# One graph network kernel: a tap step moved ahead of the first turn, input loads moved between queues, taps loaded three ahead, one copy moved to ScalarE

## The chip, the cores and the metric

The kernel runs on one core of one Trainium2 chip. The metric is the device time of one execution in microseconds. Below, PE is TensorE (matmuls and transposes), PEld its weight loads, DVE is VectorE, ACT is ScalarE, POOL is GpSimd, and SP is SyncE, which here only issues DMAs. "SPq" and "ACTq" in the profile are DMA issues of these two engines.

## The reference

The input is 128 graphs of 128 nodes with 256 features, `x (128, 128, 256)`, and an adjacency `adj (128, 128, 128)`. Two layers are computed. Cut to what matters:

```python
h  = relu(layernorm(x))                       # per node, over the 256 features
# layer 0, on every graph (channels are the features, the sequence is the nodes)
c1 = relu(bn1(conv1d(h, conv1_w)))            # 1 tap
xc = relu(bn2(conv1d(c1, conv2_w)) + h)       # 17 taps
A  = exp(-||se_i - se_j||^2) * adj            # se = h @ w_se.T + b_se
xn = A @ relu(h @ w_msg.T + b_msg)
i_r,i_z,i_n = split([xc, xn] @ w_ih.T + b_ih);  h_r,h_z,h_n = split(h @ w_hh.T + b_hh)
r, z = sigmoid(i_r + h_r), sigmoid(i_z + h_z)
x  = x + (1 - z) * tanh(i_n + r * h_n) + z * h
# layer 1
h  = relu(layernorm(x))
x  = x + sum over 5 groups g of nodes (all 25, and four subsets of them) of
         softmax(fusion_w)[g] * conv(conv(h[:, g], adj_g, W1[g], b1[g]), adj_g, W2[g], b2[g])
# conv(h, adj, W, b) = relu(D^-1/2 (adj + I) D^-1/2 (h @ W) + b), D the row sums (dinv = D^-1/2)
```

## The kernel before, in words

The graphs are cut into 32 blocks of four (`BB = 4`) and two halves of 16 blocks. The 17-tap convolution is done in a spectral form along the nodes: the taps are turned once into spectra (`vd` in DRAM), each half's activations are turned into spectra (the tile `X` in SBUF), both are multiplied per frequency, and the result (`yd`) goes to DRAM. One execution then has these stages, with the times of the profile before:

- **Heads of the first half together with the spectra of the taps, 0 to 173 us.** For each block `head_load` (L182) brings x in, `head_stats` takes mean and variance (DVE, L191 and L192; a power on POOL, L196), `head_norm` (DVE, L202) normalizes, `head_turn` transposes (eight PE transposes, L212, then relu on ACT into `ht`, L213, and a store of `ht` on the ACT queue, L214), `head_conv1` multiplies (PE, L226; add on DVE, L229; relu on ACT, L230) and `head_spectra` turns into spectra (PE, L241; copies into `X` on DVE, L247, and on ACT, L249). Between these steps `weight_spectra` runs. There are eight pieces of taps; each has four steps of 16 matmuls (two records each in the profile, L165) and four copies of the PSUM banks to the tile `sp`, three on ACT (L173) and one on DVE (L171; in the last step it is on ACT as well). After four steps `sp`, 2.56 MB, is stored to `vd` on the ACT queue (L175), and `some_spectra` starts the load of the taps after the next ones (1 MB, L155) on the ACT queue. The tile `w2` of the taps has two buffers, `sp` has two.
- **Spectral products of the first half, 173 to 277 us** (`spectral`). Per pair of frequencies p, two loads of 0.5 MB bring `v` from `vd` on SP (L294, three buffers); `s` is made on DVE (L307), `vs` on POOL (L309), then matmuls L312 and L317, and every four p a store of `yd` on the ACT queue.
- **Heads of the second half, 279 to 385 us, and its spectral products, to 489 us.**
- **The loop over blocks, to the end**: convolution output (L498 to L505), messages (L516 to L520), edges, `x_nmp` (L563 to L568), and the gates (PE, L612, by products of sums and differences of quarters: `t`, L586 to L589 for xn), with the second layer between them. The degree work of the second layer (`dinv`, L698 on) is on DVE at its start.

Order: in the first stage all engines follow the order of the text. After it SP and POOL still do, and the order of PE, DVE and ACT comes from a scheduler's cost model. DMAs signal on eight completion semaphores in turn, and an issue waits until the earlier DMA on its semaphore is complete.

`some_spectra()` does one step of 16 matmuls with its four copies. `constants()` computes the folded batch-norm vectors on DVE and POOL (L126 to L134) up to its first `yield`, and the matmuls L138 after it. `heads_begin` loads the first three blocks of the second half and takes their statistics; the generator is advanced at the frequencies p = 16, 24, 28 and so on of the first half's spectral products:

```python
        begin = heads_begin(hk, xk, 3, 1)
        amid = {p: lambda: next(begin, None) for p in range(16, NP_, 4) if p != 20}
        spectral(bp, X, 0, amid)
```

Its three loads were on the ACT queue, whose order is the scheduler's. In the profile they were issued at 142.33, 143.55 and 149.82 us, inside the heads of the first half.

Of the kernel before, what the change touches and what calls it, by code (L numbers as in the profile page):

```python
# [8 lines left out]
F32 = mybir.dt.float32  # L9
# [4 lines left out]
P = 128  # L14
# [8 lines left out]
WCH = 64  # L23
# [51 lines left out]
def gnn_kernel(ctx: ExitStack, tc: tile.TileContext, io, out0: bass.AP, out1: bass.AP):  # L75
    nc = tc.nc
# [15 lines left out]
    def bank():  # L92
        return psum.tile([P, 512], F32, tag="bank", name="bank")

    def row(name, n):

        return bass.AP(tensor=io[name].tensor, offset=io[name].offset, ap=[[0, P], [1, n]])
# [3 lines left out]
    vec = cst.tile([P, NV], F32)  # L101
# [10 lines left out]
    brz = cst.tile([P, 4], F32)  # L112

    def constant_loads():
        nc.sync.dma_start(vec, io["vec"])
        nc.sync.dma_start(wc1, io["wc1"].rearrange("(c p) o -> p c o", p=P))
        nc.sync.dma_start(fd, io["fd"])

# [30 lines left out]
    vd = dram.tile([C, D // WCH, P, LW, WCH], F32, tag="vd", name="vd")  # L149
    yd = [dram.tile([HG, 2, LW, D], F32, tag=f"yd{h}", name=f"yd{h}") for h in range(NH)]  # L150

    def taps_load(pool, c, q, queue, split=1):
        w2 = pool.tile([P, WCH // 4, P], F32, tag="w2", name="w2", bufs=2)
        for t in range(0, WCH // 4, WCH // 4 // split):
            queue.dma_start(w2[:, t:t + WCH // 4 // split], io["w2t"][:, c, q, t:t + WCH // 4 // split])  # L155
        return w2

    def weight_spectra(pool, c, q, w2):
# [21 lines left out]
    def head_load(pool, ahead, i, queue):  # L180
        xs[i] = pool.tile([P, BB, D], F32, tag="ln", name="ln", bufs=ahead)
        queue.dma_start(xs[i], x[i * BB:(i + 1) * BB].rearrange("b n d -> n b d"))  # L182

    def head_stats(wk, i, behind=None):

        mv = wk.tile([P, BB, 2], F32, tag="mv", name="mv", bufs=3)
        st = wk.tile([P, BB, 6], F32, tag="st", name="st", bufs=2)
        if behind is not None:
            nc.scalar.copy(st[:, :, 0], behind[:, :, 0])
        for b in range(BB):  # L190
            nc.vector.bn_stats(st[:, b, :], xs[i][:, b, :])  # L191
            nc.vector.bn_aggr(mv[:, b, :], st[:, b, :])  # L192
        ve = wk.tile([P, BB], F32, tag="ve", name="ve", bufs=2)
        nc.vector.tensor_scalar(ve, mv[:, :, 1], EPS, None, op0=ALU.add)  # L194
        rs = wk.tile([P, BB], F32, tag="rs", name="rs", bufs=3)
        nc.gpsimd.tensor_tensor(rs, ve, mhalf, op=ALU.pow)  # L196
        stats[i] = mv, rs
# [7 lines left out]
    def head_turn(wk, i):  # L205

        ln = xs.pop(i)
        ht = wk.tile([P, C, T], F32, tag="ht", name="ht", bufs=2)
        for c in range(C):
            ps = bank()  # L210
            for b in range(BB):
                nc.tensor.transpose(ps[:, b * N:(b + 1) * N], ln[:, b, c * P:(c + 1) * P], ident)  # L212
            nc.scalar.activation(ht[:, c, :], ps, AF.Relu)  # L213
        nc.scalar.dma_start(htd[i], ht)  # L214
        hcs[i] = ht
# [35 lines left out]
    def heads_begin(wk, xk, ahead, h):  # L251

        i = h * NBH
        for k in range(ahead):
            head_load(xk, ahead, i + k, nc.scalar)
        yield
        for k in range(3):
            head_stats(wk, i + k)
            yield
            if k < 2:  # L260
                head_norm(i + k)
        head_turn(wk, i)
# [80 lines left out]
    with front as es:  # L343
        hk = es.enter_context(tc.tile_pool(name="hk", bufs=1))
        xp = es.enter_context(tc.tile_pool(name="xp", bufs=1))
        X = xp.tile([P, C, NP_, 2, P], F32)
        order = es.enter_context(ExitStack())
        order.enter_context(tc.manual_schedule(engines={nc.gpsimd.engine}))
        sync_order = order.enter_context(ExitStack())
        sync_order.enter_context(tc.manual_schedule(engines={nc.sync.engine}))  # L350
        with ExitStack() as ws:

            ws.enter_context(tc.manual_schedule())

            xk = ws.enter_context(tc.tile_pool(name="xk", bufs=1, side="right"))
            wp = ws.enter_context(tc.tile_pool(name="wp", bufs=1))
            ahead = 5
            todo = [(c, q) for c in range(C) for q in range(D // WCH)]
            nc.scalar.dma_start(gt, io["gt"])
            taps = [taps_load(wp, *todo[0], nc.sync, split=4)]  # L360
            head_load(xk, ahead, 0, nc.scalar)
            spectra = []

            def some_spectra(k=1):
                for _ in range(k):
                    if not spectra and todo:
                        spectra.append(weight_spectra(wp, *todo.pop(0), taps.pop(0)))
                    if spectra and next(spectra[0], STOP) is STOP:
                        spectra.pop(0)
                        if len(todo) > 1:  # L370
                            taps.append(taps_load(wp, *todo[1], nc.scalar))
                        some_spectra()

            constant_loads()
            head_load(xk, ahead, 1, nc.sync)
            taps.append(taps_load(wp, *todo[1], nc.sync))
            for k in range(2, ahead):
                head_load(xk, ahead, k, nc.sync)
            nc.sync.dma_start(fw, row("fw", 5))
            head_stats(hk, 0)  # L380
            some_spectra()
            head_norm(0)
            some_spectra()
            head_turn(hk, 0)
            consts = constants()
            next(consts)
            some_spectra()
            head_stats(hk, 1)
            some_spectra()
            next(consts)  # L390
            head_norm(1)
            head_stats(hk, 2)
            some_spectra()
            heads(hk, xk, ahead, X, 0, some_spectra)
            while spectra or todo:
                some_spectra()
        gw = ctx.enter_context(tc.tile_pool(name="gw", bufs=1, side="right", reuse_waits="tile"))
        xk = es.enter_context(tc.tile_pool(name="xk1", bufs=1, reuse_waits="tile"))
        bp = es.enter_context(tc.tile_pool(name="bp", bufs=1, reuse_waits="tile"))
        idm = gw.tile([P, N], F32)  # L400
        wms = gw.tile([P, C, D + 3], F32)
        bms = gw.tile([P, D + 3], F32)
        wih = gw.tile([P, 2 * C, 3 * D], F32)
        whh = gw.tile([P, C, 3 * D], F32)
        sw = [gw.tile([P, 3, 3, P], F32, name=f"sw{k}") for k in range(3)]

        def small_loads():
            nc.sync.dma_start(idm, io["idm"])
            nc.sync.dma_start(wms, io["wms"].rearrange("(c p) o -> p c o", p=P))
            nc.sync.dma_start(bms, row("bms", D + 3))  # L410

        begin = heads_begin(hk, xk, 3, 1)
        sums = gate_weights()
        amid = {p: lambda: next(begin, None) for p in range(16, NP_, 4) if p != 20}
        spectral(bp, X, 0, amid)
        for _ in begin:
            pass

        def gate_loads():
            yield  # L420
            small_loads()
            yield
            yield
            nc.sync.dma_start(wih[:, :C], io["wih"][:D].rearrange("(c p) o -> p c o", p=P))
            yield
            yield
            nc.sync.dma_start(wih[:, C:], io["wih"][D:].rearrange("(c p) o -> p c o", p=P))
            yield
            yield
            nc.sync.dma_start(whh, io["whh"].rearrange("(c p) o -> p c o", p=P))  # L430

        loads = gate_loads()
        heads(hk, xk, 3, X, 1, lambda: next(loads, None))
        sync_order.close()
        spectral(bp, X, 1, {p: lambda: next(sums, None) for p in range(4, NP_, 4)})
        for _ in sums:
            pass
        order.close()
# [117 lines left out]
    def x_nmp(i):  # L556

        e, msg = A_s.pop(i), msgs.pop(i)
        xn = wk.tile([P, C, T], F32, tag="xn", name="xn", bufs=2)
        for c in range(C):  # L560
            ps = bank()
            for b in range(BB):
                nc.tensor.matmul(ps[:, b * N:(b + 1) * N], msg[:, b, c * P:(c + 1) * P], e[:, b, :],  # L563
                                 start=True, stop=True)
            if c:
                nc.vector.tensor_copy(xn[:, c, :], ps)  # L566
            else:
                nc.scalar.copy(xn[:, c, :], ps)  # L568
            yield
        xns[i] = xn  # L570
# [597 lines left out]
```

## Time and profile before

| | |
|---|---|
| time, median of 3 runs | 1918.53 us (1913.9 to 1918.58) |
| profiled execution: its own time | 1919.48 us |
| profiled execution: its span | 1917.7 us |
| PE busy | 1890.3 us (99% of the span) |
| DVE, ACT, POOL busy | 1303.9, 720.5, 609.1 us |
| granted PE clock, mean | 0.995 |
| DMA | 265.81 MB, 139 GB/s over the span |

The span is what the trace covers; the execution's own time is 1.8 us longer. "Busy" is the union of an engine's instructions. A line such as `L212 ... [2.63 <-issue]` says that the engine was idle for 2.63 us before this instruction, and what ended that idle time. "Chain" is the sequence of work and waits that is found by following back from the last instruction.

### The profile page before, as it was taken

The numbers are of one execution on the slowest core, as the hardware profiler recorded it, in microseconds if no ns is written. First come the engines' busy times: TensorE is split into PE (matmuls) and PEld (weight loads), VectorE is DVE, ScalarE is ACT, GpSimd is POOL, SyncE is SP. The second block draws the span as 40 slices with busy tenths as digits, with TensorE's granted clock in tenths as the row PEclk, the third lists the DMA queues.
The fourth block names the chain that finished last, engine by engine and source line by source line (L and its number), as shares of the span: only waits on it lengthen the run. The fifth ranks groups of instructions, "written<-read, shape, count | busy, mean of one in ns | idle before, by whom it ended". The sixth has DMA issues, their size and how long they took to land.

```text
span 1917.7 us, 30432 instructions
## 1 busy us (share of the span) xinstructions
PE 1890.3 (99%) x10610; PEld 1646.4 (86%) x10610; DVE 1303.9 (68%) x3247; ACT 720.5 (38%) x1555; POOL 609.1 (32%) x678
## 2 busy tenths in 40 slices
PE   8999999999999999999999999999999999999998
PEld 7888889988788888888888888888888888888887
DVE  5676557744677777777666677777756677787643
ACT  4553114411333343343343443333343434334334
POOL 1012531255234334433322233433322233443300
PEclk9999999999999999999999999999999999999999
DMA  8786896379842333333234433233334434222135
GB/s 322 288 312 226 297 311 235 121 241 306 256 117 73 74 95 76 81 90 106 71 94 97 130 97 87 73 82 108 75 90 97 144 72 107 65 78 71 36 92 151
DMA packets 248872, 265.81 MB, mean 139 GB/s; under 512 B 106866, under 2 KB 223943, under 8 KB 244239
## 3 DMA queue, kind: packets, MB, share of 16 engines
q1 hardware_dynamic: 236639, 196.70, 36.9%
q10 hardware_dynamic: 12080, 67.16, 9.0%
q8 instruction: 85, 1.39, 0.3%
q14 instruction: 68, 0.56, 0.1%
HBM read 178.66 MB, written 85.14 MB: 138 GB/s over the span
## 4 chain that ended last, share of the span: by engine, by line
PE 88%; DMA 4%; DVE 4%; issue 2%; ACT 1%; POOL 1%; SPq 0%; ACTq 0%; POOLq 0%; DVEq 0%
PE bank L612 45%; PE bank L317 6%; PE bank L516 5%; PE bank L937 5%; PE bank L877 5%; PE bank L226 4%; PE bank L312 3%; PE bank L563 3%; PE bank L498 3%; PE bank L241 3%; PE bank L165 2%; PE bank L501 1%; PE bank L788 1%; PE bank L856 1%; DMA v<-vd 1%
## 5 line engine op out<-in xcount | busy, mean ns | idle before, releaser
L612 PE MATMUL bank<-t,sw 128*128 128x256 f32 x1152 | 291.6, 380 | 0.7 <-DVE u L504 0.7
L625 POOL TENSOR_TENSOR u<-u,m 128x256 f32<-128x256 f32 x128 | 93.2, 728 | 612.7 <-ACT m L623 545.0
L612 PEld LDWEIGHTS bank<-t,sw 128*128 128x128 f32 x1152 | 215.8, 191 | 31.1 <-issue 2.3
L612 PE MATMUL bank<-t,wih 128*128 128x256 f32 x768 | 197.2, 379 | 0.0
L612 PEld LDWEIGHTS bank<-t,wih 128*128 128x128 f32 x768 | 143.4, 190 | 19.3 <-issue 0.5
L309 POOL TENSOR_TENSOR vs<-v 128x512 f32<-128x512 f32 x78 | 101.3, 1318 | 114.8 <-DMA v<-vd 49.4
L516 PE MATMUL bank<-wms,ht 128*128 128x259 f32 x512 | 124.1, 385 | 0.0
L226 PE MATMUL bank<-wc,ht 128*128 128x256 f32 x512 | 121.4, 391 | 1.6 <-ACT ht L213 1.6
L612 PE MATMUL bank<-xn,wih 128*128 128x256 f32 x384 | 114.9, 381 | 3.6 <-DVE xn L566 3.6
L612 PE MATMUL bank<-t,whh 128*128 128x256 f32 x384 | 115.0, 381 | 0.0
L612 PE MATMUL bank<-xc,wih 128*128 128x256 f32 x384 | 114.8, 381 | 0.0
L937 PE MATMUL bank<-w,hh 128*125 128x256 f32 (+9 forms) x480 | 113.5, 380 | 1.0 <-DVE hh L882 1.0
L226 PEld LDWEIGHTS bank<-wc,ht 128*128 128x128 f32 x512 | 98.0, 196 | 16.7 <-ACT ht L213 3.5
L516 PEld LDWEIGHTS bank<-wms,ht 128*128 128x128 f32 x512 | 98.3, 192 | 15.1
L612 PE MATMUL bank<-ht,whh 128*128 128x256 f32 x384 | 109.9, 380 | 0.0
L877 PE MATMUL bank<-ax,w 128*128 128x500 f32 (+8 forms) x416 | 107.0, 396 | 0.7 <-DMA w<-in_w_dram 0.7
L520 ACT ACTIVATE msg<-msg 128x512 f32<-128x512 f32 x64 | 40.3, 630 | 174.1 <-DVE msg L517 174.1
L630 DVE TENSOR_TENSOR u<-bank,u 128x256 f32<-128x256 f32 x128 | 53.7, 420 | 73.6 <-PE bank L612 73.5
L196 POOL TENSOR_TENSOR rs<-ve,mhalf 128x4 f32<-128x4 f32 x32 | 32.3, 1009 | 217.8 <-DVE ve L194 217.8
L307 DVE SCALAR_TENSOR_TENSOR s<-X 128x256 f32<-128x256 f32 x78 | 47.3, 612 | 79.4 <-PE bank L317 79.1
L937 PEld LDWEIGHTS bank<-w,hh 128*125 128x125 f32 (+9 forms) x480 | 84.3, 177 | 19.2 <-DVE hh L882 1.4
L657 ACT ACTIVATE nn<-nn,vec 128x512 f32<-128x512 f32 x64 | 46.2, 722 | 133.4 <-DVE nn L656 133.4
(187 smaller groups left out, 4279.5 us busy)
## 6 DMA issues: line engine op xcount, KB each, us to landing
v<-vd SPq DMA_DIRECT2D x80, 512.0 KB
vd<-sp ACTq DMA_DIRECT2D x8, 2560.0 KB
yd<-ys ACTq DMA_DIRECT2D x40, 512.0 KB
w<-in_w_dram SPq DMA_DIRECT2D x40, 512.0 KB
htd<-ht ACTq DMA_DIRECT2D x32, 512.0 KB
ht<-htd SPq DMA_DIRECT2D x32, 512.0 KB
ym<-yd SPq DMA_DIRECT2D x32, 512.0 KB
xt<-in_xT_dram SPq DMA_DIRECT2D x32, 512.0 KB
```

The source lines that it names most:

```text
L226: nc.tensor.matmul(pv[:, bb, :], ht[:, c, b * N:(b + 1) * N], wc1[:, c, :], start=c == 0, stop=c == C - 1)
L241: nc.tensor.matmul(ps[:, bb * 2 * LW:(bb + 1) * 2 * LW], h1[:, 2 * h + bb, c * P:(c + 1) * P], fd, start=True, stop=True)
L309: nc.gpsimd.tensor_tensor(vs, vr, vi, op=ALU.add)
L312: nc.tensor.matmul(p1[:, :D], a[:, c], vs[:, c], start=c == 0, stop=c == C - 1)
L317: nc.tensor.matmul(ps[:, k * D:(k + 1) * D], u[:, c], w[:, c], start=c == 0, stop=c == C - 1)
L498: nc.tensor.matmul(ps[:, b * N:(b + 1) * N], ym[:, b, o * P:(o + 1) * P], idm, start=b == 0, stop=False)
L516: nc.tensor.matmul(ps[:, :D + 3], ht[:, c, b * N:(b + 1) * N], wms[:, c, :], start=c == 0, stop=c == C - 1)
L563: nc.tensor.matmul(ps[:, b * N:(b + 1) * N], msg[:, b, c * P:(c + 1) * P], e[:, b, :], start=True, stop=True)
L612: nc.tensor.matmul(ps, w, d, start=n == 0, stop=n == len(pairs) - 1)
L625: nc.gpsimd.tensor_tensor(got["u4"], got["u2"], got["m5"], op=ALU.add)
L877: nc.tensor.matmul(pv[:, q - q0, :], w1s[k5 + g][:, c, q * P:(q + 1) * P], xv[:, c], start=c == 0, stop=c == C - 1)
L937: nc.tensor.matmul(ps[:n1, :D], hh[:, q, at:at + n1], w2s[k5 + g][:, q, :], start=q == 0, stop=q == HID // P - 1)
```

## The change

The edit has five parts.

1. The first block's x and `vec` change queues. `vec` goes from SP to the ACT queue behind `gt`; x of block 0 goes from the ACT queue to SP, behind the first of the four quarters of the first taps and ahead of the other three (`amid`).
2. A third step of the first taps comes ahead of the first turn, and the first part of the constants comes ahead of the second step's copies. On PE the order is 48 L165 matmuls, eight transposes L212, 16 L165, L138 (before: 32, eight, 32, L138). On DVE the constants L126 to L134 follow the first normalization, then come two copies L171, then the statistics of block 1. ACT has nine copies L173 ahead of the first relu L213 (before: six).
3. The taps have three buffers. The third taps are loaded on SP, behind x of blocks 2 to 4 and ahead of x of block 5; each later load on the ACT queue stands one piece earlier than before.
4. The three x loads of the second half go to SP, which follows the text: they stand at p = 16 of the first half's spectral products, behind v of p = 14 and ahead of v of p = 16. Their twelve pairs of statistics, which the scheduler had placed among the last heads (142 to 163 us), now stand in the spectral products on DVE, behind those of p = 11, between the `s` of p = 14, 15 and 16.
5. In `x_nmp` of block 0 alone, the second copy of `xn` is on ACT instead of DVE.

Nothing is added to or taken from the arithmetic, and PE has the same number of instructions. In the changed file the lines from L150 on stand one to three lines lower.

```diff
     def constant_loads():
-        nc.sync.dma_start(vec, io["vec"])
         nc.sync.dma_start(wc1, io["wc1"].rearrange("(c p) o -> p c o", p=P))
...
-    def taps_load(pool, c, q, queue, split=1):
-        w2 = pool.tile([P, WCH // 4, P], F32, tag="w2", name="w2", bufs=2)
+    def taps_load(pool, c, q, queue, split=1, amid=None):
+        w2 = pool.tile([P, WCH // 4, P], F32, tag="w2", name="w2", bufs=3)
         for t in range(0, WCH // 4, WCH // 4 // split):
             queue.dma_start(w2[:, t:t + WCH // 4 // split], io["w2t"][:, c, q, t:t + WCH // 4 // split])
+            if amid:
+                amid.pop()()
         return w2
...
         for k in range(ahead):
-            head_load(xk, ahead, i + k, nc.scalar)
+            head_load(xk, ahead, i + k, nc.sync)
         yield
...
             nc.scalar.dma_start(gt, io["gt"])
-            taps = [taps_load(wp, *todo[0], nc.sync, split=4)]
-            head_load(xk, ahead, 0, nc.scalar)
+            nc.scalar.dma_start(vec, io["vec"])
+
+            taps = [taps_load(wp, *todo[0], nc.sync, split=4, amid=[lambda: head_load(xk, ahead, 0, nc.sync)])]
...
-                        if len(todo) > 1:
-                            taps.append(taps_load(wp, *todo[1], nc.scalar))
+                        if len(todo) > 2:
+                            taps.append(taps_load(wp, *todo[2], nc.scalar))
...
             nc.sync.dma_start(fw, row("fw", 5))
+            taps.append(taps_load(wp, *todo[2], nc.sync))
             head_stats(hk, 0)
             some_spectra()
             head_norm(0)
-            some_spectra()
-            head_turn(hk, 0)
             consts = constants()
             next(consts)
             some_spectra()
+            some_spectra()
+            head_turn(hk, 0)
             head_stats(hk, 1)
             some_spectra()
...
-            if c:
+            if c and i:
                 nc.vector.tensor_copy(xn[:, c, :], ps)
             else:
                 nc.scalar.copy(xn[:, c, :], ps)
```

## The prediction

> **What bounds the kernel now.** I read the page first. Its first part:
>
> ```profile
> PE 1890.3 (99%) x10610; PEld 1646.4 (86%) x10610; DVE 1303.9 (68%) x3247; ACT 720.5 (38%) x1555; POOL 609.1 (32%) x678
> ```
>
> TensorE (PE) is busy for 1890.3 of 1917.7 us. The change adds and removes no matmul, so it can only win back some of the 27.4 us of idle time, and the time lost where matmuls run slower after a pause. The waits of PE, summed by line, say where that is (total, times, longest):
>
> ```profile
> PE bank L165 <- DMA gt<-in_gt_dram: 3.9, 1, 3.9
> PE bank L612 <- DVE xn L566: 3.6, 1, 3.6
> PE bank L212 <- issue: 2.6, 1, 2.6
> PE bank L165 <- DMA w<-in_w2t_dram: 2.4, 1, 2.4
> PE bank L241 <- ACT X L249: 2.3, 1, 2.3
> ```
>
> The first is the load of gt, which stays. The other four happen once each, and each part of the change sits at one of them. The timeline (start, us, engine, line, operation; in brackets the idle time before it and its releaser) gives their places:
>
> ```profile
> 10.25 2.25 PE L212 MATMUL bank<-ident,ln 128*128 128x128 f32 x8 [2.63 <-issue]
> ...
> 69.94 1.13 PE L165 MATMUL bank<-gt,w 17*128 17x80 f32 x32 [2.42 <-DMA w<-in_w2t_dram]
> ...
> 71.00 4.11 PE L241 MATMUL bank<-fd,h 128*128 128x160 f32 x16
> ...
> 82.49 2.44 PE L241 MATMUL bank<-fd,h 128*128 128x160 f32 x16
> ...
> 155.79 1.95 PE L241 MATMUL bank<-fd,h 128*128 128x160 f32 x8 [2.33 <-ACT X L249]
> 157.71 4.74 PE L226 MATMUL bank<-wc,ht 128*128 128x256 f32 x16
> ...
> 507.02 1.53 DVE L698 TENSOR_REDUCE dinv<-dga 128x53 f32<-128x1325 f32 x1 [5.18 <-DMA dga<-in_adjF_dram]
> ...
> 509.21 1.22 PE L612 MATMUL bank<-xn,wih 128*128 128x256 f32 x2 [3.58 <-DVE xn L566]
> 510.22 3.66 PE L516 MATMUL bank<-wms,ht 128*128 128x259 f32 x8
> ```
>
> See the group behind each pause: sixteen L241 took 4.11 us behind the second, 2.44 us elsewhere. A removed pause returns its own length and the slow group.
>
> [...]pauses of 2.42 and 2.33 us were followed by it (granted clock 0.66 in 70 to 75, by windows), so I count it for every pause above 2.3 us. [...]one blocked DMA issue on ACT, from 149.82 to 154.86, held the L249 copies PE waited for. [...]Here the DMA share was 0.99 over the first 25 us, so a load moved to another queue takes the same bandwidth and changes only its place.
>
> **The change part by part.**
>
> *A, the start.* PE finishes two tap steps (64 records, 3.72 us) at 7.74 and stands until 10.25, for x of block 0: landed 6.08, statistics to 8.34, POOL's power 1.03, normalization from 9.73. Now a third step stands ahead of the turn: 32 records, half of 3.72, so 1.86 us of work moved into a gap of 2.5. Then x lands earlier: ahead of it on SP is one quarter of the taps (0.26 MB) instead of, on the shared engines, about all four; 0.52 + 0.26 MB at the 352 GB/s of that window is 2.2 us after an issue near 1.3[...]: 4.5 instead of 6.08. What is late next: DVE now runs the constants (11.43 to 14.73, 3.3 us, mostly waits for POOL) ahead of the tap copies L171. Starting near 10.9 they end near 12.9 to 14; the copy that frees a bank for L138 follows, and the first L226, at 20.02 before, comes at about 17.4 to 18.5. I take 2.2. Low end 1.0 (x not earlier, the third step waits for DVE's copy), high end 2.8. Quarters 2 to 4 of the taps land up to 1.5 us (0.52 MB) later; PE has the first for 1.86 us, which may cost 0 to 0.5, inside these ends. The vec load, now on ACT behind gt, is needed at 11.4 and costs nothing; its issue (0.44 us on SP) delays no ACT work, which starts at 5.93.
>
> *B, taps three ahead.* The fifth spectra's taps were issued at 56.21 on ACT behind a 2.56 MB store and landed 13.60 us later (chain of waits). Issued one spectra earlier, at about 37, they are there by 55. Removed: 2.42 us, and 4.11 − 2.44 = 1.67 of slow clock: 4.1. Not all of it: ACT issues three DMAs in a row at 69.13, the last one taking 1.00 us, and the copies of the tap banks queue behind. I take off 0.8: 3.3. The price is 1 MB more in the first 35 us, on SP ahead of x of block 5. At 352 GB/s that is 2.8 us of all engines; windows show shares of 0.31 and 0.12 in 32 to 36, so it fits, but the first 2.56 MB store then lands near 36 to 37, and the store of ht at 36.16, which in the built program now waits for that same completion, may hold ACT for 0 to 1.5. Range of B: 1.5 to 4.3.
>
> *C, x of the second half.* Three 0.52 MB loads leave the ACT queue (issues at 142.33, 1.18 us; 143.55, 1.37 us; 149.82). In the built program the ht store issued at 154.86 waited for a v load that waits for the last tap store; without the loads it draws another completion, long passed. PE's L226 behind it ended at 162.45; without the pause, 152.21 + 2.18 + 3.45 = 157.84. Gain 4.6. The twelve statistics pairs (12 × (0.39 + 0.18) = 6.8 us) leave DVE at 142 to 163, which was not the bound, for the spectral pass, where DVE is busy for 0.18 to 0.77 of each 5 us window between 185 and 230, and are covered. The loads go to SP at 198.5, between v of p = 14 and p = 16. DMA share there is 0.92 (200 to 235); 1.57 MB is 4.5 us of all engines, against a slack of v of 2.6 to 4.2 us per pair (POOL takes v at 199.63, 204.82, 210.03, waiting for landing; PE uses vs up to 4 us later) and 0.4 us of free share per 5.2 us pair. I take a stall of 1.0 (0 to 2.5). DVE has a second way to lose: it blocks in the first statistics until x lands (206 to 209 estimated from 370 GB/s), while s of p = 14 is needed near 211. That leaves 2 us. C: 3.6, from 2.0 to 4.8.
>
> *D, first xn by ACT.* DVE sits behind dinv (L698) from 501.8 to 508.5, since its load lands at 507.02, and xn's second copy (L566) queues behind it. ACT was idle from 503.4 to 513.4, so its copy (0.59 us) is done near 502.6 and PE keeps its L612. Removed: 3.58, and the eight L516, 3.66 instead of 1.92. But t<-xn (L586 to L589, 1.7 us), and every msg and lr of DVE, still stand behind dinv. PE runs out of other work near 508 and waits for t, then for lr at L536 (DVE is packed from 507 to 532). DVE's own start is the same 507.02, so most of the 5.3 comes back as new waits. I take 1.5, from −1 (a new pause long enough to slow the clock) to 4.
>
> **Sum:** 2.2 + 3.3 + 3.6 + 1.5 = 10.6. The profiled execution took 1919.48 (span 1917.7 and 1.8 outside it), 0.95 above the median of 1918.53. 1919.5 − 10.6 = 1908.9; against the median 1907.9. I predict **1908.5**.
>
> **Rivals.** *Half of it returns* : x no earlier (A 1.0), ACT held for the tap store (B 1.5), v late (C 2.0), DVE the bound behind dinv (D 0.3). Together 4.8: 1914. For it: DMA shares of 0.9 to 1.1 in the stages that get new loads. Against it: the order of landing is better for PE in A and B. *All of it stays*: 2.8 + 4.3 + 4.8 + 4.0 = 15.9: 1903. For it: each pause has one named cause that the change removes. Against: DVE at 507. *Slower*: each DMA issue on SP or ACT waits for an earlier DMA's completion in turn (eight of them in the built programs). Shifted by the added and moved DMAs, an ACT issue can meet a 2.56 MB store (9.29 us to landing in the chain) or a tap load behind one, and ACT blocks with the tap-bank copies behind it. The place is 35 to 140 us. One such block costs what the one at 154.86 did, 2.33 of pause and 2.3 of slow clock: 4.6. Two undo nearly all of the gain, four give 1908.5 + 18.4 = 1927, and from the fourth on it is slower by more than 0.3%. In the order of the built program I find one such place (36.16, priced in B), so this is unlikely. That a part *does nothing* is possible for D alone, and is in its ends.
>
> **How the numbers follow.** The likeliest case has 0.55, half returned 0.22, all of it 0.13, slower 0.10. A measurement of this kernel can tell about 0.3%, 5.8 us, so "faster" is below 1912.8. The likeliest case is nearly all below it, half returned is below it in 1 of 4, slower lies near 1927. Faster: 0.52 + 0.06 + 0.13 = 0.71; same: 0.03 + 0.16 = 0.19; slower: 0.10. The range takes the low ends to 1903 and the half returned, with the 2 us by which single runs of before differ, to 1916.
>
> **What the profile after would show.** A: no pause at L212, first L226 near 17.5 to 18.5. B: no wait of L165 for w in 60 to 75, L241 near 65 at 2.4 us, not 4.1. C: no wait of L241 for ACT X; the L226 behind it 3.6 us; in the spectral pass, small waits of L312 for vs or L317 for s near p = 14 to 20, which must stay under 2.5 us together. D: L612's wait for xn replaced by shorter waits for t and lr around 508 to 519. I am wrong if PE's busy time is not about 1890 less some 5 us of slow matmuls, if a pause above 2.3 us appears in the spectral pass or behind an ACT issue, or if the D place still holds a slow L516.

## The result, and the profile after

The changed kernel took 1907.23 us (median of 9 runs, 1903.71 to 1911.96), the kernel before 1916.87 us beside it (9 runs). The ratio is 0.9949, with a 95% interval of 0.9936 to 0.9963: 9.8 us faster, 7.1 to 12.3. A second set of 6 runs of the same changed kernel gave 1907.44 us and a ratio of 0.9940 (0.9925 to 0.9956). The forecast was 1908.5.

The profiled execution took 1906.35 us, with a span of 1904.6. It is 13.1 us shorter than the profiled span before, so this pair of profiles shows more than the medians do. The first part of the page:

```profile
PE 1882.6 (99%) x10610; PEld 1641.7 (86%) x10610; DVE 1300.9 (68%) x3246; ACT 720.5 (38%) x1556; POOL 609.2 (32%) x678
```

PE does the same 10610 matmuls in 7.7 us less, and its idle time fell from 27.4 to 1904.6 − 1882.6 = 22.0 us. In this pair, more than half of the gain is therefore not idle time but matmuls that no longer run slowly. The trace's record of the granted clock, the share of its full clock that PE was given, shows which: before, it is at 0.5 in 40.3 to 43.8 us, 71.1 to 74.5, 156.4 to 159.8, 508.0 to 514.8 and 562.6 to 566.0, 20.5 us together; after, only in 547.4 to 554.3 us. Half of the difference, 6.8 us, is nearly all of the 7.7.

This pair overstates that share. The record lists span and granted clock of every run, and (1 − clock) × span estimates what the slow clock cost it: 8.4 us in the mean of 84 runs of before, 4.6 us in the mean of 15 runs of the changed kernel. That is 3.8 us, about a third of the gain; the larger part is idle time. The waits of PE, by line:

```profile
PE bank L166 <- DMA gt<-in_gt_dram: 4.0, 1, 4.0
PE bank L313 <- POOL vs L310: 3.8, 2, 3.0
PE bank L539 <- DVE lr L532: 2.2, 1, 2.2
PE bank L227 <- ACT ht L214: 1.6, 3, 1.1
PE bank L615 <- DVE u L507: 1.2, 1, 1.2
```

The four waits of before are gone (a short one for the taps, 0.5, now stands at the start). The wait for `lr`, behind DVE's degree work, is new; those for `vs` (v late in the spectral products) and for `u` stood in the profile before with 0.8 and 0.7 us and have grown. The timeline at the places that the prediction showed, one or two lines further down in the file than before:

```profile
10.21 1.97 PE L213 MATMUL bank<-ident,ln 128*128 128x128 f32 x8
...
64.36 2.44 PE L242 MATMUL bank<-fd,h 128*128 128x160 f32 x16
...
150.14 2.34 PE L242 MATMUL bank<-fd,h 128*128 128x160 f32 x16
152.31 3.62 PE L227 MATMUL bank<-wc,ht 128*128 128x256 f32 x16
...
203.96 1.13 PE L313 MATMUL bank<-vs,X 128*128 128x256 f32 x4 [3.04 <-POOL vs L310]
...
495.27 1.53 DVE L701 TENSOR_REDUCE dinv<-dga 128x53 f32<-128x1325 f32 x1 [4.88 <-DMA dga<-in_adjF_dram]
497.85 0.70 PE L615 MATMUL bank<-t,sw 128*128 128x256 f32 x2 [0.64 <-DVE t L590]
504.67 0.41 PE L539 MATMUL bank<-ident,lr 128*128 128x128 f32 x2 [2.20 <-DVE lr L532]
```

The transposes follow without a pause. The L242 at 64 us takes 2.44, not 4.11; L227 at 152 us takes 3.62, not 4.74. In the spectral products a pause of 3.04 us is new, and no slow clock followed it. A view of the stretch around it (length; busy us of PE, PEld, DVE, ACT, POOL with instruction counts; granted clock, DMA share, GB/s) has the clock at 1.00:

```profile
200.00:212.00 12.00, 8.96 (x42) 7.58 (x41) 6.87 (x19) 1.49 (x4) 7.90 (x6) 1.00 1.02 334
```

To put the gain in its places I cut every profile at the same events: the first conv1 matmul, the first and last copy of `k` in each half's spectral products, the first `xc` activation of block 0 and of block 3, the last one of block 31. Length of each stage in us, with the idle time of PE in it in brackets:

| stage | before | after | after, second profile |
|---|---|---|---|
| start, to the first conv1 matmul | 20.02 (6.5) | 18.05 (4.5) | 18.20 (4.8) |
| rest of the first half's heads | 156.03 (6.2) | 144.97 (1.0) | 148.65 (1.5) |
| first half's spectral products | 101.73 (1.0) | 103.33 (3.3) | 106.21 (5.9) |
| second half's heads | 110.79 (1.8) | 110.77 (1.8) | 110.79 (1.8) |
| its spectral products, to block 0 | 106.75 (0.8) | 106.75 (0.8) | 105.71 (0.0) |
| block 0 to block 3 | 99.38 (5.0) | 98.59 (5.0) | 93.94 (3.5) |
| blocks 3 to 31 | 1175.55 (0.0) | 1175.56 (0.0) | 1175.56 (0.0) |
| end | 147.45 (6.1) | 146.58 (5.5) | 146.24 (5.1) |

The last column is the same program in another execution (experiment "the changed kernel again"). Its total differs from the second column by 0.7 us, its stages by up to 4.6. One profile of one execution is not enough to size a part of a few microseconds here, so below I compare groups of profiles.

### The profile page after: what moved, and what is told of

Same layout as the page of the kernel before. It is cut to its first block, busy times and chain, and to the rows that moved or that the text cites. A ratio compares the mean times of both kernels' runs of the same rounds, so it can differ in the third digit from the quotient of the medians.

```text
span 1904.6 us, 30434 instructions
## 1 busy us (share of the span) xinstructions
PE 1882.6 (99%) x10610; PEld 1641.7 (86%) x10610; DVE 1300.9 (68%) x3246; ACT 720.5 (38%) x1556; POOL 609.2 (32%) x678
## 4 chain that ended last, share of the span: by engine, by line
PE 91%; DVE 3%; issue 2%; DMA 2%; POOL 1%; ACT 0%; SPq 0%; POOLq 0%; DVEq 0%; ACTq 0%
PE bank L615 45%; PE bank L318 6%; PE bank L519 6%; PE bank L940 5%; PE bank L880 5%; PE bank L227 5%; PE bank L313 3%; PE bank L242 3%; PE bank L566 3%; PE bank L501 3%; PE bank L166 2%; PE bank L504 1%; PE bank L791 1%; PE bank L213 1%; PE bank L859 1%
## 5 line engine op out<-in xcount | busy, mean ns | idle before, releaser
L227 PE MATMUL bank<-wc,ht 128*128 128x256 f32 x512 | 119.1, 386 | 1.6 <-ACT ht L214 1.6
L227 PEld LDWEIGHTS bank<-wc,ht 128*128 128x128 f32 x512 | 96.4, 193 | 15.7 <-ACT ht L214 3.1
L523 ACT ACTIVATE msg<-msg 128x512 f32<-128x512 f32 x64 | 40.3, 630 | 172.3 <-DVE msg L520 172.3
```

What stands on the lines that cost most here:

```text
L227: nc.tensor.matmul(pv[:, bb, :], ht[:, c, b * N:(b + 1) * N], wc1[:, c, :], start=c == 0, stop=c == C - 1)
```

## The experiments

The four kernels that follow take one part each and were run together; all their times stand beside the same 56 runs of before (median 1917.94). A profile shows one execution, and not always a typical one: of these four it was the slowest of 13 (the taps), the third slowest of 20 (x), the second fastest of 12 (the start).

**The start alone** (parts 1 and 2).

(The lines for `vec` and `amid` in `constant_loads` and `taps_load` are those of the whole change and are left out here.)

```diff
-            taps = [taps_load(wp, *todo[0], nc.sync, split=4)]
-            head_load(xk, ahead, 0, nc.scalar)
+            nc.scalar.dma_start(vec, io["vec"])
+            taps = [taps_load(wp, *todo[0], nc.sync, split=4, amid=[lambda: head_load(xk, ahead, 0, nc.sync)])]
...
-            some_spectra()
-            head_turn(hk, 0)
             consts = constants()
             next(consts)
             some_spectra()
+            some_spectra()
+            head_turn(hk, 0)
```

> The kernel before with parts 1 and 2 of the change alone (queues of the first x and of vec; third tap step and constants ahead of the first turn). Theory, parts add up: the first L226 comes 2.0 us earlier (18.05 instead of 20.02) and everything after keeps that 2.0; the 2.00 us issue stall of ACT at 37 and the slow L226 at 41 (5.1 us) stay. Time 2 us below before. Rival: the 2.45 us that the changed kernel won between 35 and 45 us, which I had not forecast, belong to the shifted start; then the shift is 4.2 to 4.4 from 45 us on and L226 there takes 3.7.

1917.5 us, ratio 0.9996 (0.9978 to 1.0013). The first conv1 matmul is at 18.08, as in the eight other profiles with this part (18.01 to 18.21): 1.9 us won, every time. At 51 us the shift is 3.1, since the slow L226 at 41 us was a fast one in this execution: neither the theory's 2.0 nor the rival's 4.2 (the experiment "the changed kernel again" takes up that place). In the time the 1.9 us can't be told from nothing.

**The taps alone** (part 3).

```diff
-        w2 = pool.tile([P, WCH // 4, P], F32, tag="w2", name="w2", bufs=2)
+        w2 = pool.tile([P, WCH // 4, P], F32, tag="w2", name="w2", bufs=3)
...
             nc.sync.dma_start(fw, row("fw", 5))
+            taps.append(taps_load(wp, *todo[2], nc.sync))
```

(and `todo[2]` in place of `todo[1]` in `some_spectra`.)

> The kernel before with part 3 alone (three tap buffers, third taps on SP, each later load one piece earlier). Theory: the wait of L165 for w at 70 us (2.42) and the slow L241 behind it (1.67) go, 4.1 us, and the unforecast 2.45 us between 35 and 45 come from here too, since the ACT queue carries one megabyte less ahead of its three issues in a row at 36: shift 6.5 us from 75 us on, time about 6.5 below before. Rival: 4.1 only, with the 2.00 us stall of ACT and the 5.1 us L226 still there.

1912.07 us, ratio 0.9958 (0.9942 to 0.9975), 8 us by the ratio and 5.9 by the medians: the only part whose gain shows in the time alone. The wait for w is gone, L241 at 69 us takes 2.44, and the slow group at 41 us is still there (5.41): the rival's picture, 4.1 us from the pause. The times moved by more. The clock lists say where part of it came from: the estimate of the slow clock's cost is 4.7 us in the mean of these 13 runs and 8.5 in the 56 of before. The rest of the first half's heads takes 151.24 (idle 4.0), 4.8 less than before; its spectral products take 105.36 (3.6), 3.6 more, with a wait for vs of 1.93.

**x of the second half alone** (part 4).

```diff
-            head_load(xk, ahead, i + k, nc.scalar)
+            head_load(xk, ahead, i + k, nc.sync)
```

> The kernel before with part 4 alone (x of the second half on SP at p = 16). Theory: 4.6 us won where L241 waited for ACT at 155 us, 3.3 lost near p = 15 to 16 where PE waits for vs behind v loads that the x loads delay, some 1.6 won back by 280 us: shift 3.0 in the block loop. Rival: the 3.0 us wait at p = 15 exists only in the shifted schedule of the whole change; alone, no wait above 1 us there and 4.6 won.

1915.64 us, ratio 0.9995 (0.9983 to 1.0008). The wait for ACT X at 155 us (2.33 before) is gone, and the spectral products lose more than that: 106.61 (4.4), with a wait for vs of 2.9 near p = 15. The rival, that this wait needs the whole change, falls. In the heads this profile shows something else, the wait for the fifth taps with what follows it:

```profile
67.66 2.01 PE L165 MATMUL bank<-gt,w 17*128 17x80 f32 x32 [2.77 <-DMA w<-in_w2t_dram]
69.60 4.63 PE L241 MATMUL bank<-fd,h 128*128 128x160 f32 x16
...
82.19 4.63 PE L241 MATMUL bank<-fd,h 128*128 128x160 f32 x16
88.69 4.99 PE L226 MATMUL bank<-wc,ht 128*128 128x256 f32 x16
96.94 2.44 PE L241 MATMUL bank<-fd,h 128*128 128x160 f32 x16
```

The order of this stretch is that of before, where the same pause (2.42) was followed by one stretch of 3.4 us at half clock. Here the clock is at 0.5 in 67.4 to 74.2 us, full for 6.8 us, and at 0.5 again from 81.1 to 91.3 us. That is some 8.5 us lost, and between the two stretches PE stood for no more than 0.27 us: the second one has no such pause ahead of it.

**xn by ACT alone** (part 5).

```diff
-            if c:
+            if c and i:
                 nc.vector.tensor_copy(xn[:, c, :], ps)
```

> The kernel before with part 5 alone (second xn of block 0 by ACT). Theory: 3.2 us won by 526 us, of which about 2.4 are lost again between 515 and 575 us, where DVE is the bound behind the degree work and the loads of dck: net 0.8, time within noise of before. Rival: [...]alone, 3 us stay.

1919.73 us, ratio 1.0002 (0.9988 to 1.0015). From block 0 to the second `xc` of block 1 the profile takes 27.70 instead of 31.24; from there to block 3 69.57 instead of 68.14. So 3.5 won, 1.4 given back: net 2.1 here, and nothing that the time can show. (The four ratios together come to 0.9951, the whole change to 0.9949; with intervals of 2.4 to 3.4 us to each side this does not prove that the parts add up.)

The next four start from the changed kernel (7 runs of before beside them, median 1916.27).

**Part 4 undone.** The edit is the one-line diff of "x of the second half alone", reversed.

> The changed kernel with part 4 undone (x of the second half on the ACT queue again). Theory: part 4 is worth what the stages show in the changed kernel, the pause at 155 us with its slow matmuls (4.6) less the 1.6 that the first half's spectral products became longer: 3.0, so about 1910 us. Rival: part 4 alone measured 1.0 us, so undoing it costs 1 us or less.

1907.85 us, ratio 0.9951 (0.9935 to 0.9967), against 0.9949 and 0.9940 of the changed kernel. By these values part 4 is worth 0.4 to 2 us, nearer to the rival; with intervals of 3 us to each side the theory's 3.0 is not excluded. The heads take 148.76 (3.8), the pause being there again, but the spectral products 104.66 (4.5): they are long without the three loads too. And no slow clock followed the pause this time. Below are first this profile, then that of "the start alone":

```profile
146.99 1.35 PE L242 MATMUL bank<-fd,h 128*128 128x160 f32 x8 [1.72 <-ACT X L250]
148.91 3.77 PE L227 MATMUL bank<-wc,ht 128*128 128x256 f32 x16 [0.57 <-ACT ht L214]
```

```profile
151.96 1.35 PE L242 MATMUL bank<-fd,h 128*128 128x160 f32 x8 [1.54 <-ACT X L250]
153.87 5.30 PE L227 MATMUL bank<-wc,ht 128*128 128x256 f32 x16 [0.56 <-ACT ht L214]
```

The same two pauses, shorter if anything in the second, cost one group 1.5 us there and nothing here. "The taps alone" has them too (1.61 and 0.56), again without a slow group (3.78).

**The x loads spread** over p = 8, 12 and 16.

```diff
-        for k in range(ahead):
-            head_load(xk, ahead, i + k, nc.sync)
-        yield
...
-        amid = {p: lambda: next(begin, None) for p in range(16, NP_, 4) if p != 20}
+        amid = {p: lambda: next(begin, None) for p in range(24, NP_, 4)}
+        for k, p in enumerate((8, 12, 16)):
+            amid[p] = lambda k=k: head_load(xk, 3, NBH + k, nc.sync)
```

> The changed kernel with the three x loads of the second half one at a time, at p = 8, 12 and 16, not all three at p = 16. Theory, the loads delay v because 1.57 MB stand ahead of one pair in one place: each alone (0.52 MB, 1.5 us) fits the slack of v of 2.6 us, the waits of PE for vs (3.8 us, longest 3.0) fall below 1 us and the first half's spectral products take 1.6 us less than 103.33. Rival, the stage has no free transfer time (DMA share 0.92) and the delay of v only moves: waits for vs of 2 us and more remain, at other p.

1905.85 us, ratio 0.9946 (0.9930 to 0.9963); spectral products 103.51 (3.1). The waits for vs fell to 1.2 us (longest 0.8), but PE stood 1.9 us at the L315 behind them. The wait changed its place and its size little: the theory's 1.6 us did not come. The rival is right that the delay moves, but not about its form, since no wait for vs reached 2 us.

**The degree work behind the messages of block 1.**

```diff
-        nc.vector.memset(dinv[:, K0:], 0.0)
+        nc.vector.tensor_scalar(dinv, lr[:, 1, 0, 3:4].to_broadcast([P, n]), 0.0, None, op0=ALU.mult)
         nc.vector.reduce_sum(dinv[:, F0:K0], a, axis=AX.X)
...
-            next(degs, None)
+            if i or turn[0] >= 2:
+                next(degs, None)
```

> The changed kernel with the degree work of the second layer held back on DVE until the messages of block 1 are through it (its zeroing reads a value of block 1's lr; the results are the same). Theory, part 5 gave little because DVE stands in dinv for 4.9 us with t, msg and lr behind it: the waits for t (0.6) and lr (2.2) go, and the loop's start to block 6 takes some 3 us less than 98.59. Rival, the degree work then comes too late for dck and block 1 to 2 stop longer: the wait of 1.2 us for u becomes 4 or more and nothing is won.

1908.79 us, ratio 0.9956 (0.9942 to 0.9971). DVE waits 2.0 us for dga, not 4.9, and PE no longer for t and lr; the stretch to block 1 falls to 24.8 us. But DVE's waits for dck rose to 5.2 us in three pieces, and the next stretch took 72.2. Nothing is won: the rival, in its mechanism. The degree work has a deadline at both ends.

**Six buffers for dck.**

```diff
-            dc = l1.tile([P, P], F32, tag="dck", name="dck", bufs=3)
+            dc = l1.tile([P, P], F32, tag="dck", name="dck", bufs=6)
```

> The changed kernel with six buffers for dck, not three. Theory: the load of dck issued at 537.92 behind the store of the first output block comes before it, DVE no longer waits 3.18 us for it at 544, PE's waits for u (1.2) and m (0.7) there and the slow matmuls behind go: about 3 us. Rival: with dck there, DVE is simply busy with other work and the wait for u stays at 1 us or more; nothing measurable.

1902.40 us, ratio 0.9924 (0.9908 to 0.9940): 3 to 5 us faster than the changed kernel. DVE's wait for dck is gone, and from the second `xc` of block 1 to block 3 it takes 64.7, not 70.5. In the changed kernel these two lines, DVE's and PE's, had shown it:

```profile
544.04 0.29 DVE L819 TENSOR_TENSOR nt<-nt,dck 125x125 f32<-125x125 f32 x1 [3.18 <-DMA dck<-dvk]
...
545.04 0.70 PE L615 MATMUL bank<-t,sw 128*128 128x256 f32 x2 [1.19 <-DVE u L507]
```

In that profile the wait of 1.2 us at PE had slow matmuls behind it (granted clock 0.50 from 547.4 to 554.3 us, some 3.4 us lost).

The last four stand beside 21 runs of before (median 1917.79).

**The changed kernel again**, unaltered.

> The changed kernel again, unaltered, beside the next three on one chip: 1907 us, ratio to before 0.995. In its profile the heads of the first half again take 145 us with 1.0 us of idle PE (before: 156, 6.2), if that gain is one of order and not of luck.

1907.44 us, ratio 0.9940 (0.9925 to 0.9956). Its heads took 148.65 (1.5), not 145. The 3.7 us lie at one place. First the changed kernel as above, then this execution of it; the first line of each is the issue of the taps on the ACT queue:

```profile
35.33 0.97 ACTq L154 DMA_DIRECT2D w<-in_w2t_dram  x1
37.03 1.12 PE L166 MATMUL bank<-gt,w 17*128 17x80 f32 x28 [0.36 <-DVE X L248]
38.08 3.72 PE L227 MATMUL bank<-wc,ht 128*128 128x256 f32 x16
```

```profile
36.55 2.10 ACTq L154 DMA_DIRECT2D w<-in_w2t_dram  x1
38.26 0.41 PE L166 MATMUL bank<-gt,w 17*128 17x80 f32 x2 [0.36 <-DVE X L248]
39.17 1.11 PE L166 MATMUL bank<-gt,w 17*128 17x80 f32 x26 [0.50 <-ACT sp L174]
40.21 5.41 PE L227 MATMUL bank<-wc,ht 128*128 128x256 f32 x16
```

The same issue of the same program took 0.97 and 2.10 us; behind the longer one PE stood twice, not once, and then lost 1.7 us in one slow group. Over all fourteen profiles: seven have an issue of 0.39 to 0.97 us there, and the group took 3.72 in each; seven have one of 1.91 to 2.23 us, and the group took 5.13 to 6.50 in six of them and 3.72 in one. That one is "part 4 undone", where PE stood 0.36 and 0.36 us; in "xn by ACT alone" it stood 0.36 and 0.34 and the group took 5.41. Kernels with and without each part are on both sides, so no part decides it alone, and what the changed kernel's profile had won at 40 us belongs in the main to that execution. Whether a part makes the long issue rarer, fourteen profiles can't say.

**Part 3 undone**: the diff of "the taps alone", reversed.

> The changed kernel with part 3 undone (two tap buffers, taps two ahead). Theory, part 3 is the bulk: alone it measured 0.9958 of the 0.9949, so undoing it costs about 8 us (1915), with the waits for w at 65 us and the slow matmuls at 40 and 70 us back. Rival, my forecast's share: the pause of 2.4 us and its slow group alone, 4 us (1911).

1909.80 us, ratio 0.9955 (0.9941 to 0.9968), against 0.9940 on the same chip: 2.4 us by the medians and 2.9 by the ratios, where alone the part gave 8 (4.8 to 11.1). The theory's 8 did not come, and the rival's 4 us lies between the two values. The pause came back as forecast, with a slow group:

```profile
65.32 1.75 PE L166 MATMUL bank<-gt,w 17*128 17x80 f32 x32 [2.17 <-DMA w<-in_w2t_dram]
67.01 4.64 PE L242 MATMUL bank<-fd,h 128*128 128x160 f32 x16
```

and the group at 38 us took 3.72 without part 3 as well, behind an issue of 0.44 us.

**The kernel before with six buffers for dck.**

> The kernel before, with six buffers for dck and nothing else. Theory, the wait for dck is independent of the change: the loop's start to block 6 gets shorter by the same 4.8 us that the changed kernel gained, 1912. Rival: without part 5, PE has stopped for xn already and DVE reaches dck later; the gain is 2 us or less.

1913.19 us, ratio 0.9970 (0.9958 to 0.9982), 5.8 us by the ratio and 4.6 by the medians: the wait for dck is independent of the change. Block 0 to block 3 takes 93.09, not 99.38.

**More v ahead**, on top of the six dck buffers.

```diff
-                    v = bp.tile([P, C, D // WCH, 4, WCH], F32, tag="v", name="v", bufs=3)
+                    v = bp.tile([P, C, D // WCH, 4, WCH], F32, tag="v", name="v", bufs=4)
...
-                vs = bp.tile([P, C, D // WCH, WCH], F32, tag="vs", name="vs", bufs=3)
+                vs = bp.tile([P, C, D // WCH, WCH], F32, tag="vs", name="vs", bufs=2)
```

> The changed kernel with six buffers for dck, and in the spectral products four buffers for v instead of three and two for vs instead of three (the memory needs it). Theory, what the x loads and the spread of landing times of v cost is a matter of how far v is loaded ahead: PE's idle time in the first half's spectral products falls from 3 to 5 us to below 1.5, and the time from 1902.4 to about 1899. Rival, the stage is short of transfer rate itself (DMA share 0.92): one pair more ahead is used up once, and the waits stay within 1 us of what they were.

1898.57 us (1894.59 to 1901.39), ratio 0.9896 (0.9879 to 0.9914): 8.9 us faster than the changed kernel beside it, and the fastest of all. PE's waits in the first half's spectral products and up to the heads behind them, first the changed kernel again, then this one:

```profile
PE bank L313 <- POOL vs L310: 5.1, 3, 2.7
PE bank L227 <- ACT ht L214: 1.1, 1, 1.1
PE bank L318 <- issue: 0.9, 1, 0.9
```

```profile
PE bank L318 <- issue: 1.8, 1, 1.8
PE bank L227 <- ACT ht L214: 1.4, 2, 1.1
```

The waits for vs are gone, and the stage takes 101.94 (1.8), as in the kernel before; the idle time is 0.3 us above the 1.5 that the theory allowed. So the rival, a stage short of transfer rate, falls in this profile: the transfers had the rate (299 GB/s in the stage at a DMA share of 0.92, against 286 and 0.87 in the changed kernel again), but three buffers did not cover their late landings. POOL's waits for the landing of v, 47.0 us between 160 and 282 us in the changed kernel again, are gone.

## Why the prediction was right, and where it was not

The sum was right: 10.6 forecast, 9.6 to 11.5 by the times. Its terms were not all, and that it came out within 1.3 us is in part luck: the heads gave some 2 us more than the forecast, the first half's spectral products took back some 2 us more. With groups of profiles in place of single ones:

**A was right**, 1.9 us for the 2.2 that I took. One step failed: x landed at 5.40, not 4.5. The 4.5 was an issue near 1.3, 2.2 us of transfer and 1 us beside it, which was my estimate and not read from a trace; the issue took 1.19 to 1.61, and from there to 5.40 it was 1.6 us beside the 2.2. The rate stayed as I had counted it: over the first 25 us the transfers ran at 358 GB/s with a DMA share of 0.97 (before 352 and 0.99), and in the first 8 us the transfers of the SP and the ACT queue took 73.7 and 4.3% of the time of the 16 engines; before, with x of block 0 on the ACT queue, 58.6 and 20.8%. Moving x ahead of three quarters of the taps brought 0.7 us, not 1.6, and the transposes started no earlier (10.21, before 10.25). PE also waited 0.54 for the second quarter of the taps, about the upper end of what I had priced. The third tap step filled the gap, and that was enough.

**B and C in the heads.** Four profiles without parts 3 and 4 (before, the start alone, xn alone, before with dck) have 154.7 to 158.6 us there, mean 156.3; six with all parts have 144.5 to 149.0, mean 146.3. That is 10.0, where I took 3.3 + 4.6 = 7.9. The difference of 2 us is not clear of the spread of so few profiles, and the six were 1.7 us faster in the mean than the medians of their kernels. What the 10.0 consists of is clear: the idle time of PE in this stage fell from 6.2 us to 1.2, and the time at half clock from a mean of 10 us (three stretches of 3.4) to 1.7 (half of one), which is worth 4.3.

C's place took 10.24 us before, from the first L241 at 152.21 to the end of L226, and 5.79 after: 4.4 won, as forecast. But I priced one slow group behind each pause, and the runs show that its cost varies: nothing behind this one in "the taps alone" and "part 4 undone", 1.7 us here, 8.5 in the profile of "x alone". In both profiles with part 3 and without part 4, the pause that C removes was 1.6 to 1.7 us and nothing slow followed. So part of what I counted for C may be won by B already; two profiles are too few to say so. Why part 3 is worth 8 us by the ratio alone and 2 to 3 in the whole change stays open; the intervals overlap.

**C's price was mis-sized: 1.0 forecast, 3 measured.** Four profiles without parts 3 and 4 have 101.1 to 102.3 in the first half's spectral products, mean 101.8; seven with part 4 and three v buffers (103.3 to 106.6) have a mean of 104.9. The step that failed is the slack of v. I read it as 2.6 to 4.2 us per pair from the moments at which POOL took v in one execution, and took one execution's values for a bound. In the second profile POOL waited up to 8.75 us for one v. The rate that I took for the landing of x, 370 GB/s, was near enough: before has 368 in 140 to 150 us and 373 in 150 to 160, the changed kernel 359 in 185 to 200, where the three loads were issued from 186.97 on and DVE had the first at 194.49. The stall was placed correctly, near p = 15. But one of my own signs of being wrong came: a pause above 2.3 us in this stage (3.04 us), and waits of 3.8 us together where I allowed 2.5. That it cost no slow clock was luck, since I had counted one behind every pause of that length. What I had not seen is that part 3 alone has the same effect (105.36; with part 4 undone, 104.66). Why, no run shows. Both kernels' v landed late in some pairs at the same order of issues; the fourth buffer cures it in the whole change.

**D was right in size for a reason that held only in part.** I expected new waits for t and lr to take back most of the 5.3 us. They were 2.8 us in the first profile (0.6 and 2.2) and 0.7 in the second. From block 0 to the second `xc` of block 1, five profiles without part 5 have 29.4 us, eight with it (the held-back degree work left out) 26.5: 2.9 won. Then from there to block 3, with three dck buffers, 67.9 without it and 69.2 with it: 1.3 given back in the stretch where DVE waits for dck. Net 1.6, forecast 1.5. That this wait takes it back is not shown: with six buffers the stretch is still longer with part 5 (64.7 twice) than without (63.85). The wait itself was in the profile before, as the 6.05 us of dck in the chain of waits, and I did not follow it.

**The slower rival did not come.** In the heads of both profiles of the changed kernel ACT waits for no transfer; the longest stop is 3.1 us in issuing three of them in a row. The case "half of it returns" was close for C and wrong for the rest; "all of it stays" was wrong at DVE and right in the heads.

## What to carry to other kernels

A pause of the busiest engine cost its own length here and, sometimes, a stretch of slow clock behind it (one group lost 1.5 us to it behind pauses of 1.54 and 0.56 us in "the start alone", none did behind 1.72 and 0.57 in "part 4 undone"). The second part was about a third of the gain, and it is the less certain one: the length of the pause did not decide whether it came. So price it as a chance, judge it by the clock of many runs and not of one profile, and price a part with the others in place. Where a load must arrive just in time, price the slowest landing and not the typical one: more buffers (v, four for three: some 4 to 5 us; dck, six for three: some 5 us) were worth about as much as the reordering. Follow a wait of the engine behind the one that you free: here DVE's wait for dck, there before the change already, was worth three times the part that led me to it.

## What the runs showed of the hardware that I had not expected

The same program, executed twice, differed by up to 4.6 us in one stage and by 0.7 in all. Three things varied: the issue of one DMA on ACT (0.97 and 2.10 us), the landing of the same transfer (dga, 7.6 and 4.8 us from its issue to the end of DVE's wait), and whether slow matmuls followed a pause.

From some 25 us on, the granted clock in the records of the profile before and of the changed kernel's first profile is either 1.0 or 0.5. The stretches at 0.5 that end before the kernel does are 3.41 us long (four times before) or 6.83 (once in each), that is one or two times 3.41; those of "x alone" above were 6.8 and 10.2 us. The full-clock stretches between those of before are whole multiples of 3.41 us too (27.31, 81.92, 348.16 and 47.79 us: 8, 24, 102 and 14 times). So the starts of before lie on a grid with a step of 3.41 us, all of them 2.8 us past a multiple of it in the time of the span; the one of the changed kernel, at 547.4, lies 1.3 us past one. A group of 16 matmuls that fell into one stretch lost about half of 3.41, 1.7 us (5.41 for 3.72 in the changed kernel again, 4.11 for 2.44 before).

What starts such a stretch stays open. Pauses of 1.54 and 0.56 us were followed by one, 1.72 and 0.57 were not; 0.36 and 0.34 were, 0.36 and 0.36 were not; 3.04 us in the spectral products were not, 2.92 us there in "x alone" were (217.6 to 221.0 us). The idle time within one step of the grid does not decide it either: 0.69 us was followed in "xn by ACT alone", 0.72 in "part 4 undone" and 1.76 in the changed kernel were not. So the count of one slow group for every pause above 2.3 us, which I took from two pauses of before (2.42 and 2.33 us), was an estimate that these runs do not bear out: slow groups stood behind far shorter pauses, and 3.04 us had none.
